# A graph network's neighbour gathers: at most four in flight instead of eight

## The chip, the cores and the metric

The kernel runs on one core of a Trainium2 chip. The metric is the device time of one execution in microseconds (us); lower is better. The time of a kernel is the median of several runs.

## The reference: what is computed

The input is a table x of 3327 nodes with 256 features and an adjacency matrix of 3327 x 3327 integers, about 0.5% of them ones: a node has some 16 neighbours, and the list of them is not known before the run.

Layer 0 is a simple attention over the graph: scores from one vector, softmax over neighbours, a weighted sum, a projection, a residual and a layer norm. Layers 1 to 3 are transformer layers whose attention sees neighbours alone:

```python
qkv = layer_norm(x, g1, be1) @ w_qkv              # 8 heads of 32
scores = jnp.einsum('nhd,mhd->hnm', q, k) * SCALE
scores = jnp.where(adj != 0, scores, -jnp.inf)
attn = jax.nn.softmax(scores, axis=-1)
out = jnp.einsum('hnm,mhd->nhd', attn, v).reshape(n, DIM)
x = x + out @ w_proj + b_proj
x = x + jax.nn.gelu(layer_norm(x, g2, be2) @ w1 + b1) @ w2 + b2
```

## The kernel before

The kernel does the attention sparsely. In a first stage it reads the adjacency matrix, computes layer 0, makes for each node the list of its neighbours, and sorts the nodes by their number of neighbours. From then on the nodes stand in 26 blocks of 128 in sorted order. Block b has room for `CAPS[b]` neighbours a node, 40 for the first block and 24 down to 10 for the others, 448 in all; a shorter list is filled up with the index of one fixed row that stands for no neighbour. (A second, dense path for other inputs is in the program and isn't entered here.)

Keys and values of all nodes lie in a table in HBM for each layer, `kv[L]`, a row of 512 floats to a node (528 in layer 1). For each of the 448 neighbour places of a layer one gather (L1226) fetches, for the 128 nodes of a block, the row of the neighbour in that place: an indirect DMA of 128 rows of 2 KB, issued from GpSimd (POOL), 1344 of them in the three layers. Up to `GS` = 4 gathers fill one tile `kv`, which is a group. The tiles come from a ring of `NBUF` = 10.

The code of one layer is the class `Layer`:

- `issue` takes the next group's tile from the ring and records its gathers. In layer 1 it also records `gather_rows` (L1186), which fetches the sorted rows of x, of the queries and of the neighbour lists of a later block into the tile `t2`, one indirect DMA a block. A layer begins with ten calls of `issue`; later `values` calls it once for every group it has used up.
- `scores` (L1248, L1249) multiplies the keys of a group with the block's query and sums over each head, on VectorE. In layer 1 ScalarE also copies the neighbours' ranks out of the gathered rows (L1252).
- `softmax` and `weights` (L1260 to L1276) are small operations for each block.
- `values` (L1289) multiplies the values of a group with the weights on VectorE; TensorE then sums them with an identity matrix into `po` (L1294). Once this product has been made, the tile is free.
- `block` and `chunk` hold the steps of the projection, the feed-forward part and the next layer's keys, values and queries. They are queued in `short` and `long` and handed out between the groups by `some`, at a rate that is worked out from their costs. In layer 3 the steps of a chunk end with stores of the output from POOL (L1439).

The order of all instructions on each engine is that of the code (`manual_schedule`); nothing reorders them. `values` runs behind `scores` by at least a block, so VectorE's work on one group stands between that on others, in an order written out in `run`. Blocks are taken in the order 25, 1, 24, 2, and so on, with block 0, the one of 40 places, as the last. A layer can begin its gathers only when all of the layer's keys and values are stored.

The framework gives each DMA that POOL issues one of eight semaphores in turn. A DMA that takes a semaphore up again waits for the one that had it before, so each waits for the eighth transfer ahead of it on POOL's queue.

Of the kernel before, what the change touches and what calls it, by code (L numbers as in the profile page):

```python
# [60 lines left out]
CB = 4  # L61

FAR = 2.0 ** 100


@with_exitstack
# [457 lines left out]
def sparse_path(ctx, tc, ins, out, dram, flag):  # L524
    nc = tc.nc
# [40 lines left out]
    class Norm:  # L566


        def __init__(self, n, name):
            self.n, self.name = n, name  # L570
            self.mv = small.tile([P, 4, 2], FP, tag="mv", name=f"mv_{name}")
# [613 lines left out]
    def gather_rows(b):  # L1185
        nc.gpsimd.indirect_dma_start(  # L1186
            out=t2[:, b, :], out_offset=None, in_=t1,
            in_offset=bass.IndirectOffsetOnAxis(ap=perm[:, b:b + 1].bitcast(U32), axis=0))
# [11 lines left out]
    class Layer:  # L1200
        def __init__(self, L, w, nxt):
            self.L, self.w, self.nxt = L, w, nxt
            self.groups = [g for b in ORDER for g in slots[b]]
            self.issued = 0
            self.tiles, self.sc, self.wp, self.q, self.po = {}, {}, {}, {}, {}
            self.rows = 0

            self.short, self.long = [], []
            self.rate = self.credit = 0.0

        def issue(self):

            if self.issued == len(self.groups):
                return
            L, W = self.L, KVW[self.L]
            b, s0 = self.groups[self.issued]
            self.issued += 1
            while L == 1 and self.rows < min(NB, ORDER.index(b) + 3):
                gather_rows(ORDER[self.rows])
                self.rows += 1  # L1220
            n = min(GS, CAPS[b] - s0)
            t = ring.tile([P, GS * KVW[1]], FP, tag="kv", name=f"kv_{L}_{b}_{s0}")
            t = t[:, :GS * W].rearrange("p (s c) -> p s c", c=W)
            for s in range(n):
                k = 2 * D + s0 + s
                nc.gpsimd.indirect_dma_start(  # L1226
                    out=t[:, s, :], out_offset=None, in_=kv[L],
                    in_offset=bass.IndirectOffsetOnAxis(ap=t2[:, b, k:k + 1].bitcast(U32), axis=0))
            self.tiles[b, s0] = t


# [4 lines left out]
        def scores(self, b, s0):  # L1236
# [4 lines left out]
            if s0 == 0:  # L1241
                self.sc[b] = work.tile([P, LMAX, HEADS], FP, tag="sc", name=f"sc_{L}_{b}")
                if L == 1:
                    nc.vector.tensor_scalar(pad[b],
                                            t2[:, b, 2 * D:2 * D + S].bitcast(I32),
                                            0.0, FAR, ALU.is_equal, ALU.mult)
            k = t[:, :n, :D]
# [6 lines left out]
        def softmax(self, b):  # L1254
# [5 lines left out]
            nc.vector.tensor_tensor_reduce(  # L1260
                sc, sc, pad[b][:, :, None].to_broadcast([P, S, HEADS]), 1.0, FAR,
                ALU.add, ALU.min, mx)
# [305 lines left out]
```

## Time and profile before

| what | value |
|---|---|
| median of 5 runs | 3343.92 us (3343.54 to 3346.32) |
| the profiled execution | 3337.6 us |
| its span in the trace | 3335.8 us |
| mean granted TensorE clock | 0.797 |
| TensorE (PE) busy | 2136.0 us, 64% |
| VectorE (DVE) busy | 1957.7 us, 59% |
| GpSimd (POOL) busy | 1358.9 us, 41% |
| ScalarE (ACT) busy | 766.7 us, 23% |
| DMA queue of POOL (q0) | 370.26 MB, 39.4% of 16 engines' span |

How to read it: busy times are summed over the span, and the engines work beside each other, so none of these shares says alone what the span is made of. A GpSimd gather counts as busy while it is being issued; its data arrives later. The first stage ends at about 630 us; the gathers of layer 1 start at 634.4 us, those of layer 2 at 1569.8, and the last gather of layer 3 at 3232.7. A wait in these views is an idle time of an engine just ahead of an instruction, put down to what ended it.

### The profile page before, as it was taken

The numbers are of one execution on the slowest core, as the hardware profiler recorded it, in microseconds if no ns is written. First come the engines' busy times: TensorE is split into PE (matmuls) and PEld (weight loads), VectorE is DVE, ScalarE is ACT, GpSimd is POOL, SyncE is SP. The second block draws the span as 40 slices with busy tenths as digits, with TensorE's granted clock in tenths as the row PEclk, the third lists the DMA queues.
The fourth block names the chain that finished last, engine by engine and source line by source line (L and its number), as shares of the span: only waits on it lengthen the run. The fifth ranks groups of instructions, "written<-read, shape, count | busy, mean of one in ns | idle before, by whom it ended". The sixth has DMA issues, their size and how long they took to land.

```text
span 3335.8 us, 22700 instructions
## 1 busy us (share of the span) xinstructions
PE 2136.0 (64%) x6859; PEld 1143.4 (34%) x6859; DVE 1957.7 (59%) x4063; ACT 766.7 (23%) x1335; POOL 1358.9 (41%) x1461
## 2 busy tenths in 40 slices
PE   4566666235678787675346887878743656766666
PEld 4444444113333333343123333333421323333334
DVE  3977774554656655643546657575445646556553
ACT  3344442001222222221012222222310211211111
POOL 3000000364555555421654555456035565556450
PEclk9676667567888888887678898889866878878888
DMA  4223321464555555532654555556145454545450
GB/s 177 101 109 109 120 77 52 144 185 136 161 153 164 165 161 163 148 90 78 177 146 143 150 157 172 148 156 180 29 133 163 139 162 138 161 139 163 136 142 13
DMA packets 144482, 453.73 MB, mean 136 GB/s; under 512 B 29521, under 2 KB 40156, under 8 KB 141021
## 3 DMA queue, kind: packets, MB, share of 16 engines
q0 software_dynamic: 113056, 370.26, 39.4%
q1 hardware_dynamic: 9834, 53.90, 4.6%
q10 hardware_dynamic: 21458, 28.02, 2.3%
q8 instruction: 56, 0.92, 0.1%
q14 instruction: 78, 0.64, 0.1%
HBM read 420.64 MB, written 31.42 MB: 136 GB/s over the span
## 4 chain that ended last, share of the span: by engine, by line
issue 15%; PE 15%; POOL 13%; DVE 10%; another core or an unknown queue 5%; DMA 4%; ACT 2%; DVEq 0%; POOLq 0%; SPq 0%; ACTq 0%
POOL kv L1226 12%; PE po L1294 5%; DMA kv<-kv,t 3%; PE pu L1373 3%; DVE kv L1248 3%; PE py L1396 2%; DVE vw L1289 2%; DVE sc L1249 2%; PE pk L1426 2%; PE pq L1426 1%; PE po L1330 1%; PE po L1319 1%; PE py L1389 0%; DVE t L1414 0%
## 5 line engine op out<-in xcount | busy, mean ns | idle before, releaser
L1226 POOL DMA_INDIRECT kv<-kv,t x1344 | 1273.0, 947 | 1254.2 <-issue 559.8
L1294 PE MATMUL po<-vw,s_ident 128*128 128x512 f32 (+1 forms) x1380 | 786.8, 708 | 484.0 <-DVE vw L1289 344.4
L1294 PEld LDWEIGHTS po<-vw,s_ident 128*128 128x128 f32 x1380 | 295.8, 227 | 847.4 <-issue 489.9
L1248 DVE TENSOR_TENSOR kv<-kv,q 128x1024 f32<-128x1024 f32 (+3 forms) x363 | 413.0, 1138 | 158.4 <-ACT q L1234 71.3
L1334 DVE TENSOR_TENSOR t<-t,po 128x256 f32<-128x256 f32 x78 | 32.8, 420 | 667.6 <-PE po L1330 287.8
L1249 DVE TENSOR_REDUCE sc<-kv 128x32 f32<-128x1024 f32 (+3 forms) x363 | 414.1, 1141 | 12.4
L1289 DVE TENSOR_TENSOR vw<-kv,w 128x1024 f32<-128x1024 f32 x333 | 371.7, 1128 | 75.5 <-remote 70.8
L1373 PE MATMUL pu<-fT,s_w 128*128 128x512 f32 (+3 forms) x768 | 322.5, 554 | 43.9 <-issue 22.7
L1396 PE MATMUL py<-gT,s_w 128*128 128x512 f32 (+2 forms) x672 | 285.8, 553 | 2.5 <-issue 2.1
L1373 PEld LDWEIGHTS pu<-fT,s_w 128*128 128x128 f32 x768 | 154.3, 212 | 200.0 <-issue 155.0
L1379 ACT ACTIVATE gT<-pu,pvb 128x512 f32<-128x512 f32 (+3 forms) x192 | 115.8, 608 | 308.3 <-PE pu L1373 181.7
L702 POOL MEMSET s_abf<- 128x1 bf16 x26 | 2.6, 103 | 435.5 <-PE s_ptb L714 252.3
L1312 ACT COPY o<-po 128x512 f32<-128x512 f32 x78 | 45.6, 585 | 554.2 <-PE po L1294 263.6
L1396 PEld LDWEIGHTS py<-gT,s_w 128*128 128x128 f32 x672 | 128.2, 193 | 126.1 <-issue 108.7
L1319 PE MATMUL po<-s_ident,o 128*128 128x128 f32 x624 | 98.2, 307 | 97.0 <-ACT o L1312 67.6
L714 PE MATMUL s_ptb<-s_ident_bf,s_abf 128*128 128x128 bf16 x676 | 76.3, 290 | 114.4 <-ACT s_aT L715 83.3
L1319 PEld LDWEIGHTS po<-s_ident,o 128*128 128x128 f32 x624 | 88.8, 214 | 139.8 <-ACT o L1312 88.5
L1426 PE MATMUL pk<-s_w_qkv,nT 128*128 128x512 f32 x208 | 117.8, 696 | 10.6 <-issue 7.0
L1328 PE MATMUL po<-bias,s_ones_bf 96*128 96x256 bf16 x78 | 22.7, 291 | 158.9 <-ACT oT L1324 86.7
L1330 PEld LDWEIGHTS po<-s_w_proj,oT 128*128 128x128 f32 x312 | 60.3, 215 | 186.8 <-issue 179.5
L724 DVE MAX8 cand<-s_v 128x8 f32<-128x208 bf16 x416 | 117.6, 360 | 0.9
L1324 ACT COPY oT<-po 128x256 f32<-128x256 f32 x78 | 29.0, 372 | 369.4 <-remote 210.5
(284 smaller groups left out, 2485.6 us busy)
## 6 DMA issues: line engine op xcount, KB each, us to landing
s_a<-in_adj_dram SPq DMA_DIRECT2D x25, 1663.5 KB
kv<-kv,t POOLq DMA_INDIRECT x1344
kv<-kvr ACTq DMA_DIRECT2D x52, 256.0 KB
kv<-s_kvr ACTq DMA_DIRECT2D x26, 256.0 KB
s_w<-in_L_gnn_w_dram SPq DMA_DIRECT2D x6, 1024.0 KB
t<-ql ACTq DMA_DIRECT2D x6, 592.0 KB
t<-s_x ACTq DMA_DIRECT2D x6, 512.0 KB
s_w_qkv<-in_L_gnn_w_qkv_dram SPq DMA_DIRECT2D x3, 768.0 KB
```

What stands on the lines that cost most here:

```text
L724: nc.vector.max(out=self.cand[:, s, :], in_=v[:, s, :])
L1226: nc.gpsimd.indirect_dma_start(out=t[:, s, :], out_offset=None, in_=kv[L], in_offset=bass.IndirectOffsetOnAxis(ap=t2[:, b, k:k + 1].bitcas ...
L1248: nc.vector.tensor_mul(k, k, self.q[b][:, None, :].to_broadcast([P, n, D]))
L1249: nc.vector.tensor_reduce(self.sc[b][:, s0:s0 + n, :], k.rearrange("p s (h d) -> p s h d", d=HD), AX.X, ALU.add)
L1289: nc.vector.tensor_mul(vw[:, :n * D].rearrange("p (s h d) -> p s h d", h=HEADS, d=HD), v, self.wp[b][:, s0:s0 + n, :, None].to_broadcast([ ...
L1294: nc.tensor.matmul(self.po[b][:, :m], ident, vw[:, s * D:s * D + m], start=(s0 + s == 0), stop=(s0 + s + 2 >= S), skip_group_check=True)
L1319: nc.tensor.matmul(pt[:, k * P:(k + 1) * P], c["o"][:, k0:k0 + P], ident, start=(h == 0), stop=(h == 1))
L1330: nc.tensor.matmul(ps, c["oT"][:, k * P:(k + 1) * P], w["w_proj"][:, k, :], start=False, stop=(k == 1))
L1373: nc.tensor.matmul(c["pu", f][:, :n], w["w1"][:, e, f * P:(f + 1) * P], c["hT"][:, e, :n], start=(e == 0), stop=(e == 1))
L1379: nc.scalar.activation(g[:, :n], c.pop(("pu", f))[:, :n], AF.Gelu_apprx_tanh, bias=w["b1"][:, f:f + 1])
L1396: nc.tensor.matmul(c["py"][e][:, :n], w["w2"][:, f, e * P:(e + 1) * P], g[:, :n], start=(f == 0), stop=last)
L1426: nc.tensor.matmul(ps[:, :c1 - c0], c["hT"][:, e, j * P:(j + 1) * P], nxt["w_qkv"][:, e, c0:c1], start=(e == 0), stop=(e == 1))
```

## The change

Each gather of a layer is kept in a list. From the fifth on, a gather is made to wait for the landing of the gather four places ahead of it in its layer. The row gathers of layer 1 and the stores of layer 3 are neither counted nor made to wait in this way. As the framework knows that what lies further back has then landed too, it leaves out the waits for the eighth transfer ahead where the new ones cover them.

```diff
@@ -61,6 +61,9 @@
 FAR = 2.0 ** 100
+
+FLIGHT = 4
+WAIT = mybir.DependencyInfo(mybir.DependencyClass.Sync, mybir.DependencyReason.DATA)
@@ -1204,6 +1207,7 @@
             self.rows = 0
+            self.flight = []
@@ -1223,9 +1227,14 @@
             for s in range(n):
                 k = 2 * D + s0 + s
-                nc.gpsimd.indirect_dma_start(
+                got = nc.gpsimd.indirect_dma_start(
                     out=t[:, s, :], out_offset=None, in_=kv[L],
                     in_offset=bass.IndirectOffsetOnAxis(ap=t2[:, b, k:k + 1].bitcast(U32), axis=0))
+
+                if len(self.flight) >= FLIGHT:
+                    tc.add_manual_dep(got.ins, self.flight[-FLIGHT].ins.name, WAIT,
+                                      reason="gathers in flight")
+                self.flight.append(got)
             self.tiles[b, s0] = t
```

## The prediction, made before the changed kernel ran

> **What bounds the kernel now.** I read the chain that ended last first, then the groups, then the waits, then the POOL timeline and the chain inside one stretch.
>
> From the page, the chain by engine and the gather's row (busy us and mean ns of one, then idle time before it):
>
> ```profile
> issue 15%; PE 15%; POOL 13%; DVE 10%; another core or an unknown queue 5%; DMA 4%; ACT 2%; DVEq 0%; POOLq 0%; SPq 0%; ACTq 0%
> L1226 POOL DMA_INDIRECT kv<-kv,t x1344 | 1273.0, 947 | 1254.2 <-issue 559.8
> ```
>
> No engine owns the path. The gathers are on it with 13%, and the time in which the chain waits for transfers to land is 4%. So a gather matters in some stretches and not in others. The waits tell in which (us in total, times, longest):
>
> ```profile
> POOL kv L1226 <- issue: 559.8, 1164, 17.5
> POOL kv L1226 <- DVE vw L1289: 388.2, 71, 18.2
> DVE kv L1248 <- DMA kv<-kv,t: 47.9, 20, 7.1
> POOL kv L1226 <- DMA kv<-kv,t: 14.6, 48, 0.3
> ```
>
> The first row is in the main the pause that follows each gather. Apart from it POOL waits most for VectorE to free a buffer of the ring (388.2 us): there it has run ahead. VectorE waits for gathers only 20 times. The last row is the present limit: each gather already waits for the eighth transfer ahead of it on POOL's queue, and such a wait was never longer than 0.3 us, which is the usual pause between two gathers. The limit of eight costs nothing.
>
> The question is how much earlier than needed the fourth gather ahead lands. The POOL timeline at the start of layer 2, where POOL runs without pause (start, length, idle before):
>
> ```profile
> 1591.94 0.95 POOL L1226 DMA_INDIRECT kv<-kv,t  x1 [0.30 <-DMA kv<-kv,t]
> 1593.19 0.95 POOL L1226 DMA_INDIRECT kv<-kv,t  x1 [0.30 <-issue]
> 1594.44 0.95 POOL L1226 DMA_INDIRECT kv<-kv,t  x1 [0.30 <-issue]
> 1595.69 0.95 POOL L1226 DMA_INDIRECT kv<-kv,t  x1 [0.30 <-issue]
> 1596.94 0.94 POOL L1226 DMA_INDIRECT kv<-kv,t  x1 [0.30 <-DMA kv<-kv,t]
> ```
>
> One gather starts every 1.25 us (0.95 of work, 0.30 of pause), so a gather's fourth predecessor began 5.0 us before it: 1596.94 - 1591.94. The chain in the same stretch shows how long a gather takes from POOL's start to landing, and how soon POOL goes on after a wait:
>
> ```profile
> 1573.22 3.71 DMA kv<-kv,t
> 1576.93 0.02 issue
> 1576.95 0.04 POOLq L1226
> 1577.00 0.91 POOL kv L1226
> ...
> 1578.21 3.63 DMA kv<-kv,t
> ...
> 1581.96 4.55 DMA kv<-kv,t
> ...
> 1588.20 3.61 DMA kv<-kv,t
> ...
> 1605.69 3.41 DMA kv<-kv,t
> ```
>
> Landing takes 3.4 to 4.6 us, and POOL goes on 0.07 us after a landing (1576.93 to 1577.00). The new wait therefore delays a gather only if the landing takes over 5.0 - 0.07 = 4.93 us. Put another way: 3.65 us of landing at one start per 1.25 us is 2.9 gathers in flight, under four already.
>
> [...]
>
> **The change, part by part.**
>
> *Instructions.* In the built program the order on all five engines is unchanged. Each gather but the first four of a layer waits on the semaphore of the fourth gather ahead in place of the eighth transfer ahead. Where a gather needs two transfers' semaphores, a separate wait instruction stands ahead of it: 22 more of them on POOL. One took 0.04 us (POOLq in the chain above) and fits in the 0.30 us pause: the start at 1596.94 follows such a wait (1596.88) and is still 1.25 us after 1595.69. 22 x 0.04 = 0.9 us of sequencer time, hidden by the pause; without that cover 0.9 us.
>
> *What is queued behind the wait.* POOL is in order: behind a waiting gather stand the next gathers, in layer 1 the row gathers (L1186), in layer 3 the stores of the output (L1439). VectorE's product (L1248) waits for a group of four. The ring holds ten groups, so in most of a layer POOL's work is wanted tens of us later; that hides short waits. Without that cover, at a layer's start, POOL's delay reaches VectorE in full.
>
> *Where landings exceed 4.93 us.* For each gather I took the time from its start to the last increment recorded on its semaphore. Increments are missing from many records; among the 164 gathers with all 16 recorded the median is 3.66 us and the 90th percentile 4.43. As a second measure, the time at which queue q0 had moved all bytes up to a gather's end has a median of 2.89 and a 95th percentile of 3.49 us, and full records lie 0.75 us after it (0.52 to 1.25). By either measure long landings stand in few places:
>
> (a) The start of layer 1, 634 to 645 us, where weights load at the same time: 5.9 to 6.6 us for the first seven gathers. The DMA share there is full and POOL has nothing to hide behind:
>
> ```profile
> 634.40:645.00 10.60, 0.00 (x0) 0.00 (x0) 3.33 (x8) 0.00 (x0) 8.16 (x9) 0.50 1.04 383
> ```
>
> (the last two columns: DMA share, GB/s). Gather 5 started at 639.38; gather 1 started at 634.38 and landed 6.58 later, so 5 now starts at 640.96 + 0.07 = 641.03, 1.65 later. 6, 7 and 8 follow at 1.25, their own predecessors having landed. Gather 9 waits for 5, now at 641.03 plus its landing: 6.31 us as recorded, or about 5.2 if the weights are through by then: start at 647.4 or 646.3 in place of 644.41, so 3.0 or 1.9 later. I take 1.9, as the share falls to 0.87 after 645. Ends: 1.1 (with every landing held to 6.0 us) and 3.0.
>
> VectorE waits for gathers between 656 and 682 (five waits, 10.3 us in that window), each after POOL pacing at 1.25 us, so the delay passes through: **+1.9 us**. By 692 POOL is forty gathers ahead and waits 12.5 us for a buffer, but VectorE's releases have moved with it.
>
> (b) The last dozen gathers of each layer (1433 to 1445, 2321 to 2333, 3215 to 3221): 5 to 10 us. Stepping through the recorded starts with the cap gives 5.2, 3.8 and 0.6 us of POOL delay. It is hidden: in layer 1 the last gather would start at 1449.9 in place of 1444.7, while VectorE takes its group at 1475.66; in layers 2 and 3 the last groups are taken at 2365.3 and 3263.0, over 20 us after landing. POOL's next gathers are a layer away. If that cover were gone: 9.6 us.
>
> (c) The starts of layers 2 and 3: landings of 3.4 to 4.9 us, no wait. **0**.
>
> (d) All else: POOL is ahead. **0**; as bounds, one missed wait of a few tenths per layer start up to +2 us, and below nothing only through less traffic beside the weights, at most the 1 us by which they might land earlier; the first product (648.37) comes after small loads but the next ones wait for gathers anyway.
>
> *Sum.* 1.9 + 0 + 0 + 0 = +1.9 us. The profiled execution took 3337.6 us, 1.8 around its span of 3335.8; with the change 3339.5. The median of the runs lies 6.3 us above that execution, so 3343.92 + 1.9 = **3345.8 us**.
>
> **Rivals.**
>
> *A: the cap never binds in what matters* (the shift of (a) is lost in VectorE's own pauses). For it: 2.9 in flight; the row gathers and stores are not counted, so five can be up. Against: VectorE is waiting for exactly these gathers. 3343.9 us.
>
> *B, the slower side: the landing that POOL sees is over 4.93 us in the POOL-paced starts of the layers.* Its place is the first forty gathers of each layer, where VectorE follows POOL directly. For it: missing records make landings look short, and one of 4.55 stands in the chain. At 5.6 us POOL's pace would be 5.6 / 4 = 1.40 in place of 1.25, so 3 x 40 x 0.15 = 18 us, plus the 1.9: 3364 us. It decides from 4.93 us on. Against: the byte count of q0, which misses nothing, puts the 95th percentile at 3.49 + 0.75 = 4.2.
>
> *C, faster: fewer gathers beside other transfers let those land earlier.* For it: DMA share 1.04 at 634 to 645. Against: with 2.9 in flight there is little to take away, and what lands earlier is followed by gather-paced work. The first row of weights-bound VectorE waiting is 12.6 us at 641; half of it would give 3337.6 us.
>
> **How the numbers follow.** Chances: forecast 0.60, A 0.20, B 0.14, C 0.06. Forecast and A lie within 0.2% (6.7 us, about what a measurement of this kernel can tell from no change). A small part of the forecast's case ends over it and a small part of C's under it does not: faster 0.05, same 0.79, slower 0.16. Leaving out most of B and C, the range runs from 3340 (runs 0.4 under the median, less contention, re-timed engines) to 3356 (the ends of (a) and (d), the 9.6 of (b) in part, B at its mildest).
>
> **What would show it.** Right: the gathers' waits for gathers grow from 14.6 us by some 10 to 13, with the longest about 1.7 to 2, at 639, 644 and each layer's end; the pace at 1570 to 1605 stays 1.25 us; VectorE's waits for gathers stay near 48 us, 1 to 3 more. Wrong: a pace over 1.25 us in the starts of layers 2 and 3 (B), or the first product well before 648 us and a shorter layer 1 (C).

## The result, and the profile after

| | this kernel | kernel before |
|---|---|---|
| median of the runs measured side by side | 3325.26 us (3294.43 to 3339.32, 22 runs) | 3345.83 us (3330.5 to 3366.36, 43 runs) |
| ratio, 95% interval | 0.9929, 0.9913 to 0.9944 | |
| profiled execution | 3345.44 us | 3337.6 us |

The change made the kernel 0.7% faster, where 1.9 us slower was forecast. The ratios in this document compare runs taken side by side, so they can differ by up to 0.001 from the quotient of the two medians (here 0.9939). The profiled execution of the changed kernel took longer than every one of its timed runs, so its span can't be set against that of before; the trace is used below for the order and the length of single steps.

The page's chain and the gather's row, after (busy us and mean ns of one, then idle time before it and what ended most of it):

```profile
PE 34%; DVE 27%; another core or an unknown queue 14%; issue 11%; ACT 5%; POOL 4%; DMA 4%; DVEq 0%; ACTq 0%; POOLq 0%; SPq 0%
L1230 POOL DMA_INDIRECT kv<-kv,t x1344 | 1273.3, 947 | 1264.9 <-issue 488.6
```

The gathers cost what they did (1273.3 us busy, 947 ns each). One entry should stop a reader: "another core or an unknown queue" holds 14% of the chain, and this program runs on one core. It held 5% in the chain that the prediction showed. The waits after (us in total, times, longest):

```profile
POOL kv L1230 <- issue: 488.6, 1126, 16.0
POOL kv L1230 <- DVE vw L1298: 424.1, 74, 20.6
DVE t L1343 <- PE po L1339: 364.7, 44, 28.5
DVE t L1343 <- remote: 223.1, 15, 19.1
...
ACT oT L1333 <- remote: 138.9, 15, 23.0
...
DVE kv L1257 <- DMA kv<-kv,t: 58.1, 25, 6.9
...
POOL kv L1230 <- DMA kv<-kv,t: 37.8, 88, 2.3
```

The last row is the new wait: 37.8 us in place of 14.6, 88 times in place of 48, the longest 2.3 in place of 0.3. VectorE's waits for gathers went from 47.9 to 58.1 us. Both rows are worse than before, and neither can have made the kernel faster. The rows marked "remote" are waits that ended by a signal whose sender the profile can't name. (A signal here is the increment of a semaphore on which an instruction of another engine waits; the trace records it with its time.) No other core takes part in this program.

**What the prediction had passed over.** The same rows stood in the profile of before, and I had not followed them:

```profile
DVE t L1334 <- PE po L1330: 287.8, 34, 26.1
...
ACT oT L1324 <- remote: 210.5, 17, 24.1
DVE t L1334 <- remote: 200.4, 13, 18.1
```

L1334 is VectorE's add after the projection of a block; L1330 is the projection on TensorE. The timeline of before shows one such wait (start, length, engine and operation, idle time before):

```profile
690.27 1.91 PE L1330 MATMUL po<-s_w_proj,oT 128*128 128x256 f32 x4
...
703.05 0.42 DVE L1334 TENSOR_TENSOR t<-t,po 128x256 f32<-128x256 f32 x1 [18.05 <-remote]
```

TensorE's product ends at 690.27 + 1.91 = 692.2. VectorE, idle for 18.05 us, adds it at 703.05. For the 10.9 us between the two, TensorE, ScalarE and VectorE do nothing at all; only POOL issues gathers. VectorE waits for nothing else that the trace shows, and the trace's record of the increment that TensorE makes after this product stands at 702.95, 0.1 us before the add. So VectorE went on at once when the signal came, and the signal came 10.8 us after the product's end. I call this a late signal. The ends of matmuls are modelled in these profiles, so the trace can't tell whether TensorE sends its signal late or itself ends late.

To count them I took, from the trace's records, three handoffs from TensorE to an engine (projection to the add on VectorE, transposition and sum to their copies on ScalarE), 234 in all, and for each the time from the later of "product ended" and "the consumer came free" to the consumer's start. In before it is 530 us in sum, 23.4 at the most, and over 1 us 67 times. In the changed kernel it is 505 us, 21.3 and 63. (Delays can overlap, so the sum isn't time lost by the kernel.) Only TensorE's signals were found late: in the same trace none of 156 handoffs from ScalarE to TensorE (the two copies to the transposition and the projection) and none of 298 from VectorE to TensorE (weighted values to their sum) is late by over 0.15 us. The trace of before also holds only 15,699 records of semaphore updates; below it turns out that some 31,000 were due.

### The profile page after: what moved, and what is told of

It reads as the page before. It is cut to its first block, busy times and chain, and to the rows that moved or that the text cites. A ratio compares the mean times of both kernels' runs of the same rounds, so it can differ in the third digit from the quotient of the medians.

```text
span 3343.6 us, 22722 instructions
## 1 busy us (share of the span) xinstructions
PE 2136.6 (64%) x6859; PEld 1147.1 (34%) x6859; DVE 1959.1 (59%) x4063; ACT 767.2 (23%) x1335; POOL 1359.2 (41%) x1461
## 4 chain that ended last, share of the span: by engine, by line
PE 34%; DVE 27%; another core or an unknown queue 14%; issue 11%; ACT 5%; POOL 4%; DMA 4%; DVEq 0%; ACTq 0%; POOLq 0%; SPq 0%
PE po L1303 9%; PE py L1405 5%; PE pu L1382 5%; DVE kv L1257 5%; DVE vw L1298 4%; DVE sc L1258 4%; POOL kv L1230 4%; DMA kv<-kv,t 3%; DVE cand L727 2%; PE pk L1435 2%; PE po L1328 2%; PE po L1339 1%; ACT s_abf L708 1%; PE s_pk L994 1%
## 5 line engine op out<-in xcount | busy, mean ns | idle before, releaser
L1230 POOL DMA_INDIRECT kv<-kv,t x1344 | 1273.3, 947 | 1264.9 <-issue 488.6
L1435 PE MATMUL pk<-s_w_qkv,nT 128*128 128x512 f32 x208 | 117.7, 695 | 10.7 <-issue 5.5
L717 PEld LDWEIGHTS <-s_abf 128*128 128x128 bf16 x676 | 65.3, 135 | 128.9 <-issue 95.0
```

What stands on the lines that cost most here:

```text
L717: nc.tensor.transpose(pt[:, m, :], self.abf[:, k * P:(k + 1) * P], ident_bf)
L1230: got = nc.gpsimd.indirect_dma_start(out=t[:, s, :], out_offset=None, in_=kv[L], in_offset=bass.IndirectOffsetOnAxis(ap=t2[:, b, k:k + 1]. ...
L1435: nc.tensor.matmul(ps[:, :c1 - c0], c["hT"][:, e, j * P:(j + 1) * P], nxt["w_qkv"][:, e, c0:c1], start=(e == 0), stop=(e == 1))
```

## The experiments

Each kernel ran beside the kernel before on the same chip, and each ratio is against that. Two chips gave times of about 3370 us for the kernel before, two others 2904 us. That difference is the main finding, so the chip stands with each run. "Pace" is the mean distance of gather starts that follow each other within 2.3 us; lateness is the sum over the 234 handoffs and the number over 1 us; records are those of semaphore updates in the trace. The traces of the kernel before on these four chips weren't kept; where a trace of before is named, it is that of the first measurement, whose chip isn't known.

| run | edit | chip | kernel before, us | this, us | ratio (95%) | pace, us | lateness, us | records |
|---|---|---|---|---|---|---|---|---|
| e1_cap4_again | cap of 4 | 8 | 2903.59 | 2909.69 | 1.0014 (0.9999 to 1.0029) | 1.28 | 11, 0 | 31,030 |
| e2_cap8 | cap of 8 | 8 | 2903.59 | 2904.37 | 0.9997 (0.9985 to 1.0008) | 1.26 | 12, 0 | 31,027 |
| e3_cap6 | cap of 6 | 8 | 2903.59 | 2905.72 | 0.9999 (0.9988 to 1.0010) | 1.26 | 11, 0 | 31,030 |
| e4_cap3 | cap of 3 | 8 | 2903.59 | 2995.59 | 1.0308 (1.0291 to 1.0325) | 1.40 | 11, 0 | 31,026 |
| e5_cap4_chip2 | cap of 4 | 3 | 3374.05 | 3366.68 | 0.9970 (0.9956 to 0.9985) | 1.27 | 522, 61 | 15,358 |
| e6_cap8_chip2 | cap of 8 | 3 | 3374.05 | 3375.34 | 1.0014 (1.0001 to 1.0027) | 1.26 | 564, 62 | 15,317 |
| e7_cap4_body | cap of 4, not in block 0 | 3 | 3374.05 | 3368.39 | 0.9989 (0.9974 to 1.0003) | 1.27 | 534, 60 | 15,525 |
| e8_cap3_chip2 | cap of 3 | 3 | 3374.05 | 3114.86 | 0.9229 (0.9202 to 0.9256) | 1.40 | 203, 43 | 18,760 |
| e9_pause_half | small memset, every 2nd gather | 9 | 2905.13 | 2902.66 | 0.9993 (0.9983 to 1.0003) | 1.26 | 12, 0 | 31,718 |
| e10_pause_each | small memset, every gather | 9 | 2905.13 | 2906.27 | 1.0006 (0.9995 to 1.0017) | 1.26 | 11, 0 | 32,373 |
| e11_cap2 | cap of 2 | 9 | 2905.13 | 3584.05 | 1.2331 (1.2308 to 1.2354) | 1.58 | 8, 0 | 31,030 |
| e12_cap3_again | cap of 3 | 9 | 2905.13 | 2997.19 | 1.0305 (1.0285 to 1.0324) | 1.39 | 11, 0 | 31,027 |
| e13_rate_137 | memset 128x160 f32 | 10 | 3375.42 | 3264.70 | 0.9677 (0.9631 to 0.9722) | 1.37 | 386, 70 | 17,454 |
| e16_rate_143 | memset 128x240 bf16 | 10 | 3367.89 | 3100.52 | 0.9214 (0.9181 to 0.9246) | 1.44 | 166, 41 | 19,987 |
| e14_rate_150 | memset 128x320 bf16 | 10 | 3375.42 | 3071.70 | 0.9105 (0.9074 to 0.9135) | 1.50 | 11, 0 | 30,161 |
| e17_rate_150 | the same again | 10 | 3367.89 | 3071.63 | 0.9119 (0.9096 to 0.9142) | 1.50 | 11, 0 | 30,155 |
| e15_half_bytes | half the row, layers 2 and 3 | 10 | 3367.89 | 3374.37 | 1.0020 (1.0006 to 1.0034) | 1.26 | 498, 59 | 14,475 |

### Other limits, and a chip without late signals

The first four kernels change one number of the changed kernel; the cap of eight keeps the edit but should bind hardly anywhere.

```diff
-FLIGHT = 4
+FLIGHT = 8        # e2; 6 in e3, 3 in e4; e1 leaves 4
```

What was expected, of e1, e2, e3 and e4 in turn:

> The changed kernel once more (cap of four), for a second trace and its times beside the others on one chip. All theories: about 0.993 of the kernel before (0.991 to 0.995). Theory 'traffic' (fewer gathers in flight relieve the DMA engines where gathers pile up: the first ten us of layer 1 and the last dozen gathers of each layer) expects the gain in those three or four stretches of the trace. Theory 'timing' (the small shifts re-time TensorE against VectorE, and the gain is not tied to the number in flight) expects it spread over the layers or not visible in one trace.

> The same edit with a cap of eight, which the kernel before has already by its semaphores: the same code path in the framework, no tighter limit. Theory 'traffic': 1.000 of the kernel before (0.998 to 1.002). Theory 'artifact' (the gain comes from how the added dependency changes the waits in the built program, not from the cap): 0.993 like the changed kernel. Theory 'timing': anything between 0.993 and 1.005.

> A cap of six, which binds only where landings take over 7.4 us (six starts at 1.25 us, less 0.07): the last gathers of layers 1 and 2, and not the start of layer 1 (6.6 us at most). Theory 'traffic' with the layers' ends as its place: 0.993 to 0.997; with the start of layer 1 as its place: 1.000. Theory 'timing': no order among caps of 8, 6, 4, 3.

> A cap of three: the third gather ahead began 3.75 us before, and landing takes 3.65 us in the median, so about half of the waits end late by some tenths of a us in the POOL-paced starts of layers. By my working of the recorded landings that is 3 x 40 gathers x about 0.15 us = 18 us more in those starts, little elsewhere. Theory 'traffic': the gain of the cap of four less these 18 us, so 0.998 to 1.000 of the kernel before. Theory 'timing': 1.005 or any value near it, as the 18 us stand alone. If fewer in flight were better by itself all over the layers (less interference between transfers): under 0.993.

On this chip the kernel before took 2903.59 us, some 440 us less than in the first measurement, and the gain of the cap of four was gone: 1.0014, about 4 us slower by the ratio (0.0014 x 2903.59). Caps of six and eight make no difference. The stages show where the 440 us went: up to the first gather of layer 1 all traces take 633 to 637 us, while layers 1, 2 and 3 take 935, 891 and 875 us in before and 786, 781 and 691 in e2. So the loss lies in the gathering layers alone. TensorE's mean granted clock is lower in before too (0.797 against 0.833 in e2), but its busy time differs by only 89 us (2136.0 and 2047.4), so that alone doesn't make up the 440. The add after the same projection, in the timeline of e2:

```profile
684.00 0.36 DVE L1269 CUSTOM_DVE_ANT_1 sc<-sc,pads 128x192 f32<-128x192 f32 x1
...
684.28 0.41 DVE L1343 TENSOR_TENSOR t<-t,po 128x256 f32<-128x256 f32 x1
```

No idle time stands before it: VectorE comes to it out of other work. The longest lateness in e1 and e2 is 0.1 us, and the chain of e1 has no unknown queue:

```profile
PE 38%; DVE 26%; DMA 15%; POOL 9%; issue 9%; ACT 4%; DVEq 0%; ACTq 0%; POOLq 0%; SPq 0%
L1230 POOL DMA_INDIRECT kv<-kv,t x1344 | 1273.5, 948 | 848.9 <-issue 337.4
```

Both traces hold about 31,030 semaphore records, with all 16 increments of each of the 1344 gathers. Here, then, late signals and missing records go together. The chain also has DMA at 15%, where it had 4%: with signals on time the other engines catch up with the gathers. The waits of e1, with the cap of four:

```profile
DVE kv L1257 <- DMA kv<-kv,t: 150.5, 74, 7.1
...
POOL kv L1230 <- DMA kv<-kv,t: 80.2, 199, 2.8
```

and of e2, with a cap that hardly binds:

```profile
DVE kv L1257 <- DMA kv<-kv,t: 132.8, 72, 7.1
...
POOL kv L1230 <- DMA kv<-kv,t: 35.0, 115, 0.3
```

The cap of four holds POOL back by 45 us more and VectorE by 18 us more. The first forty gathers of layer 1 take 54.5 us against 51.5; of layer 2, 50.3 against 49.6; of layer 3, 49.0 against 48.7.

The cap of three missed my estimate. On this chip it costs 92 us by the medians; by the traces of e4 and e2 it is 104 us, of which layer 3 has 69 (760 us against 691). Its waits:

```profile
DVE kv L1257 <- DMA kv<-kv,t: 258.8, 117, 7.0
POOL kv L1230 <- DMA kv<-kv,t: 249.5, 378, 4.8
```

VectorE's waits for gathers nearly double. At a cap of three the limit is at landing divided by three, 3.65 / 3 = 1.22 us, and any landing over 3 x 1.25 - 0.07 = 3.68 us binds. I had counted that for the starts of layers only. There it came out (the first forty gathers of the three layers take 18.5 us more than in e2, 18 were expected), but the rest of layer 3 lost far more.

### The same on a chip with late signals

These four ran together on another chip. The third leaves the last block of each layer, the one with 40 places, without a cap, to see whether the gain comes from the gathers of the layers' ends:

```diff
-                if len(self.flight) >= FLIGHT:
+                if b and len(self.flight) >= FLIGHT:      # e7
```

The expectations, of e5, e6, e7 and e8:

> The changed kernel (cap of four) again, to see whether the -0.7% of the first measurement or the 1.001 of the second comes back. Theory 'late signals' (in the first measurement TensorE's results reached the engines that wait for them up to 23 us late while gathers ran, with over half of the semaphore records missing; fewer transfers in flight shorten those delays a little): where such delays appear in the trace, 0.993; where they don't, 1.000 to 1.003. Theory 'traffic' (the DMA engines themselves are relieved): 0.993 in either.

> A cap of eight, the limit that is there anyway. All theories but 'artifact of the build': 1.000 (0.998 to 1.002), with or without late signals.

> A cap of four except for the gathers of block 0, the last 40 of a layer, where landings are long: their own gathers wait as in the kernel before. If the layers' ends are the place of a gain, it is gone: 1.000. If late signals are shortened all over the layer, the gain stays: 0.993. Where there are no late signals: 1.001, like the whole cap of four, as the last gathers are used over 20 us after they land.

> A cap of three again. Without late signals 1.031 as measured before (POOL's pace is set by landing / 3 and the other engines wait for it). With late signals the rest of the kernel is slower and POOL has more time, so less is lost by the pace, and more is won if it is the number in flight that delays the signals: 0.99 to 1.015.

Here the signals are late again (522 and 564 us), half the records are missing, and the gain is back: 0.9970 with a cap of four. A cap of eight, the same program text with another number, gives 1.0014. The gain is therefore not an accident of how the edited program is built. The cap of three, which cost 3% on the other chip, gains 7.7% here: 259 us, far outside the 0.99 to 1.015 that I expected. Its waits:

```profile
DVE kv L1257 <- DMA kv<-kv,t: 197.3, 88, 7.1
POOL kv L1230 <- DMA kv<-kv,t: 178.5, 248, 5.0
DVE t L1343 <- remote: 102.8, 9, 20.2
...
ACT oT L1333 <- remote: 80.7, 14, 13.7
```

VectorE waits more for gathers, and yet the kernel is faster, since the lateness fell from 564 (cap of eight) to 203 us. Whatever makes signals late, a limit of three gathers in flight lessened it here. For the cap of four the sums are lower too (505 against 530 at first, 522 against 564 here), but each is from one trace, and this difference isn't shown to be more than chance.

Where the cap of four earns its part stays open: without block 0 the ratio is 0.9989, with it 0.9970, and the two intervals overlap. The gain also differs between measurements: 0.9929 at first and 0.9970 here, with intervals that don't meet.

### Number in flight, rate, or timing?

A cap of three changes three things: fewer gathers are in flight, gathers start at a lower rate (a mean of 1.40 us apart in place of 1.26), and everything is timed anew. A pause between gathers without a cap changes rate and timing alone. The first try:

```diff
+            idle = big.tile([P, 1], FP, name="idle")
...
+                if s % 2 == 0:                            # e9; e10 leaves this out
+                    nc.gpsimd.memset(idle, 0.0)
                 nc.gpsimd.indirect_dma_start(
```

> No cap beyond the eight of before, but a tiny POOL memset (128x1) ahead of every second gather, so that gathers start further apart: about 1.4 us on average in place of 1.25 (a memset of 0.1 us with a pause of 0.2 to 0.3 of its own). Theory 'rate' (signals come late where gathers follow each other at 1.25 us; it is the rate of landings that matters, and the caps of 3 and 4 act by slowing it): with late signals 0.92 to 0.94 of the kernel before, like the cap of three. Theory 'number' (it is how many transfers are in flight at once): the median landing of 3.65 us at 1.4 us still leaves up to eight where landings are long: 0.98 to 1.00. Without late signals, both: 1.02 to 1.04 by POOL's pace.

> The same memset ahead of every gather: starts about 1.55 us apart. Theory 'rate': with late signals, these all but gone and POOL's pace the bound: 1344 x 0.3 us = 400 us more of POOL's time in all, so 0.93 to 0.97 of the kernel before there. Theory 'number': 1.00 or more. Without late signals: 1.08 to 1.12.

> A cap of two: the pace becomes the landing of 3.7 us over 2 = 1.86 us. 1344 gathers then take about 2500 us of POOL; with the first stage (634 us) and two gaps of some 105 us between layers and the end of 80 us that gives about 3420 us on any chip: 1.01 to 1.02 of a kernel before at 3350 to 3375 us, 1.17 to 1.18 of one at 2904 us. Late signals, if they follow the rate or the number in flight, are gone, and the trace keeps nearly all semaphore records.

> A cap of three, for comparison on the same chip: 0.923 with late signals, 1.031 without.

The pause missed its aim, as the POOL timeline of e10 shows:

```profile
1450.15 0.95 POOL L1229 DMA_INDIRECT kv<-kv,t  x1 [0.19 <-issue]
1451.09 0.12 POOL L1228 MEMSET idle<- 128x1 f32 x1
1451.40 0.94 POOL L1229 DMA_INDIRECT kv<-kv,t  x1 [0.19 <-issue]
```

The memset takes 0.12 us and the idle time shrinks from 0.30 to 0.19, so the pace stays 1.25 us. This chip also had no late signals. What these four kernels do show is the price of the caps where signals are on time: three costs 3.05% (as on chip 8), two costs 23%, with gathers at a median of 1.99 us apart (1.86 us, and 17 to 18%, had been expected).

So the pause has to be longer. On a chip with late signals, three lengths:

```diff
+            idle = big.tile([P, 160], FP, name="idle")    # e13; 240 of BF in e16, 320 of BF in e14 and e17
...
+                nc.gpsimd.memset(idle, 0.0)
                 nc.gpsimd.indirect_dma_start(
```

> No cap beyond the eight of before; ahead of each gather a POOL memset of 128x160. The 128x1 memset of e10 stood in the pause between gathers and left the pace at 1.25 us; one of 128x160 should take about 0.23 us and make it 1.37 us, the mean pace of the cap of three. Theory 'rate': with late signals 0.92 to 0.94 of the kernel before, like the cap of three. Theory 'number': 0.98 to 1.01. Without late signals: 1.02 to 1.03 for either, as POOL's pace is on the path.

> A POOL memset of 128x240 ahead of each gather, no cap: about 1.43 us apart. With late signals: between 0.968 and 0.9105; if the change is a threshold, near 0.91 with hardly any late signal, and otherwise near 0.94. Without late signals: 1.03 to 1.05.

> The same with a memset of 128x320 (about 0.37 us): a pace of 1.50 us. Theory 'rate': with late signals these are rarer still, but the pace takes over: 0.93 to 0.96. Theory 'number': 1.00 to 1.04. Without late signals: 1.05 to 1.08.

> 1.50 us apart again. With late signals 0.91. Without: on the chip with late signals none was left and the kernel took 3072 us, so the same 3070 us are to be expected here, against 2904 before: 1.055 to 1.06.

The POOL timeline of e14 (one gather now starts each 1.50 us):

```profile
1601.06 0.95 POOL L1229 DMA_INDIRECT kv<-kv,t  x1 [0.17 <-issue]
1602.01 0.39 POOL L1228 MEMSET idle<- 128x320 bf16 x1
1602.56 0.95 POOL L1229 DMA_INDIRECT kv<-kv,t  x1 [0.16 <-issue]
```

With no limit beyond the kernel before's own, the time falls with the pace: 0.968 at 1.37 us, 0.921 at 1.44, 0.911 and 0.912 at 1.50. The lateness falls along with it: 386, 166 and 11 us, from some 500 (498 in e15 below, on the same chip at the old pace). At 1.50 us no handoff is late by over 1 us and no wait of the trace ends "remote". Not all records are back: e14 has 30,161, and e10, with as many memsets and its signals on time, has 32,373, so 7% are still missing. The sizes were not foreseen: for 1.37 us a theory of the rate had 0.92 to 0.94, for 1.50 us 0.93 to 0.96. VectorE's longest sum is then a plain one:

```profile
DVE kv L1251 <- DMA kv<-kv,t: 304.5, 135, 7.6
...
DVE t L1337 <- PE po L1333: 215.8, 37, 10.9
```

VectorE waits 304.5 us for gathers, six times what it waited before, and the kernel is 304 us faster. So gathers further apart are enough; a limit isn't needed.

The trace of before shows the same inside one run. Its 234 handoffs can be grouped by the number of gathers that started in the 20 us before TensorE's product ended:

| gathers in the 20 us before | handoffs | late by over 1 us | mean lateness, us |
|---|---|---|---|
| under 8 | 49 | 0 | 0.05 |
| 8 to 11 | 86 | 6 | 0.35 |
| 12 to 14 | 59 | 27 | 2.66 |
| 15 or 16 | 40 | 34 | 8.49 |

In e2, where signals are on time, no group has a late one, though 133 of the handoffs there follow on 15 gathers or more. So a run of gathers at full pace comes ahead of most late signals, within one kernel and without any edit. One control is missing: no kernel with memsets at an unchanged pace ran on a chip with late signals.

### Rate of completions, or of bytes?

A lower rate also moves fewer bytes in a microsecond. The last kernel keeps the pace and halves the bytes in layers 2 and 3: the table holds only the keys there, and the values aren't fetched (the weights multiply the keys in their place).

```diff
-KVW = {1: 528, 2: 512, 3: 512}
+KVW = {1: 528, 2: 256, 3: 256}
...
-            v = t[:, :n, D:2 * D].rearrange("p s (h d) -> p s h d", d=HD)
+            v = t[:, :n, D:2 * D] if L == 1 else t[:, :n, :D]
+            v = v.rearrange("p s (h d) -> p s h d", d=HD)
...
-                nc.scalar.dma_start(kv[L + 1][b * P:(b + 1) * P, :], kvr)
+                nc.scalar.dma_start(kv[L + 1][b * P:(b + 1) * P, :], kvr[:, :D])
```

> In layers 2 and 3 only the keys are stored and gathered (128 rows of 1 KB), and values multiplies them in place of the values, so the output leaves the values out; the number of gathers, their rate and all other instructions stay, layer 1 is unchanged. With late signals: if completions matter, late signals in layers 2 and 3 as before (layers of about 890 and 875 us, 0.99 to 1.00); if bytes matter, they go there, and these layers take about 780 and 690 us, so 0.91. Without late signals: 0.98 to 1.00[...].

The three layers in e15 (stretch, length, then busy time and number of instructions of TensorE, its weight loads, VectorE, ScalarE and POOL, then clock, DMA share, GB/s; the third stretch ends at 3220, ahead of the end of layer 3):

```profile
634.00:1577.00 943.00, 624.29 (x1659) 309.13 (x1659) 524.77 (x921) 202.87 (x464) 445.86 (x472) 0.81 0.52 146
1577.00:2489.00 912.00, 621.25 (x1659) 309.04 (x1659) 525.21 (x899) 192.24 (x346) 424.66 (x449) 0.82 0.26 71
2489.00:3220.00 731.00, 433.25 (x1100) 208.45 (x1101) 430.53 (x641) 119.11 (x204) 415.24 (x437) 0.78 0.28 78
```

The traffic is 71 and 78 GB/s where layer 1, unchanged, has 146; layer 2 still takes 912 us (891 in before), and layer 3, to the end, 875 (875 in before). Gathers land after 2.73 us in place of 3.65, so only 2.73 / 1.25 = 2.2 are in flight, where the kernel before has 2.9. The lateness stays at 498 us, of which the two layers with half rows have 333 (372 in before), and the waits without a named sender stay with it:

```profile
ACT oT L1325 <- remote: 193.9, 17, 17.7
DVE t L1335 <- remote: 191.4, 11, 22.0
```

Fewer bytes gain nothing, and fewer gathers in flight at an unchanged pace gain nothing. So traffic and number in flight fail at e15, and the way the program is built at e6. A mere change of timing would have to give ordered gains at three pauses, and the same one twice at 1.50 us. Of these, the rate of gathers is what fits all runs, the cap of three only roughly (below). What in the rate counts isn't separated: the issue on POOL, the reading of 128 rows and the increments that follow all come at the same rate.

### What a gather's rate is made of, and what stays open

With each gather come 16 increments of a semaphore (e1 has 16 recorded for each of its 1344 gathers). That makes 16 / 1.26 = 12.7 increments in a microsecond before, and 16 / 1.50 = 10.7 in e14. The lateness ends somewhere between e16's 16 / 1.44 = 11.1 and 10.7.

What delays the signals isn't shown. Missing records come with late signals, but not one for one. Traces with late signals have 38% or more of their records missing, and those of the chips without late signals hold nearly all of theirs, yet e14 and e17 miss 7% and have no late signal. And in the trace of before signals from VectorE and ScalarE come on time though their records are also missing in part: for 3169 updates by VectorE's instructions 2535 records are there, for 1209 by ScalarE's 882, and for 1246 by TensorE's 1022. Nor does any run here bear on why two chips have late signals and two have none.

Two smaller points stay open. The cap of three reaches 0.923 at a mean pace of 1.40, where the pauses of 1.37 and 1.44 give 0.968 and 0.921, a mean of the two of 0.945; its median is 1.25, so its spacing is uneven, and whether that or the limit adds something wasn't tried. And where in a layer the cap of four gains is not settled (e7).

### A version faster than both

Where signals are late, the kernel before with a pause that makes 1.50 us between gathers beats both kernels: 3071.7 us, 0.911 of the kernel before, in two measurements. (The changed kernel didn't run on that chip; its best ratio elsewhere is 0.993.) Where signals are on time it wasn't measured. As its trace has no late signal left, its 3072 us should be near its time on the other chips too; against 2904 us that would be 1.058, an estimate which takes the chips to be alike otherwise.

## Why the prediction failed, by its steps

**The sum's sign failed at one step.** It is the last one, (d): "below nothing only through less traffic beside the weights, at most the 1 us". The reason given for excluding a larger gain was that POOL is ahead, so that holding it back can give nothing. The runs showed a second way in which gathers bear on the rest: where signals are late, gathers that follow each other closely delay TensorE's signals (on chip 10 by 498 us in sum at a pace of 1.26 us, e15, and by 11 at 1.50, e14). In the first measurement the kernel before had up to 23.4 us of delay in a single handoff, and each lower rate that was tried by a pause on such a chip gave some of it back. The cap of four makes the mean distance of gathers 1.27 in place of 1.26 us only, and gains 0.7% (0.3% on chip 3); the pause to 1.37 us gains 3.2%, of which an even share for 0.01 us of 0.11 would be 0.3%, as an estimate. That the cap gains by its lower rate is inferred from these runs, not shown: its own few long waits (below) are the only place where it changes the rate, and the lateness of its trace falls by 25 us only.

**The signs had been in view.** The prediction's first fence shows "another core or an unknown queue 5%", on one core, and it is not explained there. It notes that "Increments are missing from many records" and treats this as a flaw of the measure. And of VectorE it says that it "waits for gathers only 20 times", from which it follows that POOL is ahead. On the chips without late signals VectorE waits 72 times and 132.8 us (e2). POOL was ahead since all others were held up.

**Steps that held.** (a) The first waits after, in the POOL timeline of the changed kernel:

```profile
634.34 0.94 POOL L1230 DMA_INDIRECT kv<-kv,t  x1 [1.63 <-issue]
...
638.09 0.94 POOL L1230 DMA_INDIRECT kv<-kv,t  x1 [0.30 <-issue]
641.32 0.94 POOL L1230 DMA_INDIRECT kv<-kv,t  x1 [2.28 <-DMA kv<-kv,t]
642.57 1.03 POOL L1230 DMA_INDIRECT kv<-kv,t  x1 [0.30 <-issue]
...
647.16 0.95 POOL L1230 DMA_INDIRECT kv<-kv,t  x1 [0.30 <-issue]
```

The fifth gather starts at 641.32 (641.03 was worked out) and the ninth at 647.16 (between 646.3 and 647.4). The sixth follows it by 1.25 us, at 642.57 (640.63 in before), so the fifth's wait moves the gather behind it too. The first forty gathers take 54.2 us in place of 51.7: +2.5, within the ends of 1.1 to 3.0, where 1.9 was taken.

(b) At the end of layer 1:

```profile
1437.27 0.94 POOL L1230 DMA_INDIRECT kv<-kv,t  x1 [0.87 <-DMA kv<-kv,t]
1438.52 0.94 POOL L1230 DMA_INDIRECT kv<-kv,t  x1 [0.30 <-issue]
1440.52 0.94 POOL L1230 DMA_INDIRECT kv<-kv,t  x1 [1.06 <-DMA kv<-kv,t]
...
1449.48 0.94 POOL L1230 DMA_INDIRECT kv<-kv,t  x1 [0.67 <-DMA kv<-kv,t]
```

Six gathers between 1437 and 1450 wait clearly longer than the usual 0.30 us, 4.1 us over it in sum (5.2 was stepped out), and the last starts at 1449.48 (1449.9).

(c) The starts of layers 2 and 3 take 0.7 and 0.1 us more for forty gathers; 0 was taken, and the +2 us that (d) allowed for covers it. The pace of 1.25 us stays.

**Terms that were too small.** The waits of gathers for gathers grew by 23 us in the changed kernel's trace and by 45 us from e2 to e1, where 10 to 13 were expected; VectorE's waits for gathers grew by 10 and 18 us, where 1 to 3 were expected. Where signals are on time, all this comes to about 4 us (1.0014, interval -0.3 to +8.4 us). That agrees with the forecast's mechanism and sign, but the interval takes in both no effect and the 1.9 us; the cover was thinner than I took it to be.

**The rivals.** A (no effect) can't be told from the forecast where signals are on time (e1), and doesn't hold where they are late. B (landings over 4.93 us, a slower pace at the layers' starts) is not what the cap of four does; a cap of three does it, at a pace of 1.40, and only where signals are on time does it cost 3%. C had the sign of the result, by "less traffic" at the start of layer 1. Its sign of being right, a first product well before 648 us, didn't come (647.45 us against 648.37), and e15 takes half of the traffic of two layers away and gains nothing.

## What to carry to other kernels

Read "remote" or "unknown queue" in a program on one core as an unexplained hold-up, which it was here (200.4 us of VectorE's idle time in before), not as a gap in the records: take one such wait, find the producer's end and the consumer's start in the timeline, and see whether anyone was busy between. Where a resource looks ahead of all others, ask whether those others are being held up by something that the resource itself causes, before a change to it is costed at nothing. A gain from throttling one queue is to be tested by throttling it in another way, by halving its bytes, and on more than one chip, since here a cap of three was 3% slower on two chips and 7.7% faster on a third.

## What the runs showed of the hardware

- The same kernel took 2904 and 2905 us on two chips and 3368 to 3375 us on two others. The traces reach the first gather of layer 1 at 633 to 637 us whether signals are late or not, so the difference lies in the layers that gather. In the slower trace of before (3337.6 us), signals from TensorE reached a waiting engine up to 23.4 us late, and 15,699 semaphore records stand where some 31,000 were due. Signals from VectorE and ScalarE to TensorE were on time there (454 handoffs, none late by over 0.15 us).
- On chip 10 signals were late at 12.7 gather increments in a microsecond, less so at 11.1, and not at 10.7 (lateness 498 us in e15, 166 in e16, 11 in e14).
- An indirect gather of 128 rows of 2 KB occupied POOL for 0.95 us, and at full pace one started each 1.25 us (before, 1591.94 to 1596.94 us). In the chain of before it landed 3.4 to 4.6 us after its start (at the start of layer 2). A memset of 128x1 between two gathers (0.12 us, e10) cost nothing (pace 1.25 us, ratio 1.0006); one of 128x320 bf16 (0.39 us, e14) cost 0.25 us of pace.
- With signals on time, a cap of six (e3, 0.9999) was as good as eight (e2, 0.9997); four cost about 0.14% (e1, interval -0.01 to 0.29), three 3% (e4, e12), and two 23% (e11).
